# An expert tile's activations transposed between the halves of the next tile's gate and up products

## The chip, the cores and the metric

The kernel runs on one core of a Trainium2 chip. The engines named below are TensorE (PE in the profile, with PEld for its weight loads and PEldq for its sequencer), VectorE (DVE), ScalarE (ACT), GpSimd (POOL) and SyncE (SP). The metric is the device time of one execution in microseconds (us); everything is f32. Before the change three runs took 1644.12, 1644.21 and 1644.91 us, a median of 1644.21 us.

## The reference

The input is one sequence of 2048 tokens of width 512. A Mamba-2 block with a gated MLP is added to the layer-normed input, and then a mixture of experts is added to that. Only the mixture of experts is touched by the change:

```python
x = x + attn_ref(layernorm(x), ...)      # mamba2, then the gated MLP
x = x + ffn_ref(layernorm(x), Wr, Wg, Wu, Wd)
...
probs = softmax(x @ Wr)                  # 8 experts
topk_w, topk_idx = top_k(probs, 2)       # two experts for a token
g = einsum("bsh,ehi->besi", x, Wg)       # h = 512, i = 352
u = einsum("bsh,ehi->besi", x, Wu)
h = silu(g) * u
y = einsum("besi,eih->besh", h, Wd)
out = einsum("bse,besh->bsh", combine, y)
```

The kernel computes only the chosen pairs: 4096 pairs of a token and an expert, sorted by expert and cut into tiles of 128 rows that each belong to one expert. With each expert's last tile padded this makes NS = 39 tiles at most, and the program always runs 39.

## The kernel before

The first 1284 us or so are the Mamba block and the MLP, which the change does not touch. The MLP of the last 512 tokens ends with their routing (`route`, lines 496 to 584: layer norm, router product, the two best experts by VectorE arithmetic, and lists of the pairs). A table of the first eight tiles is made earlier, from the first 1536 tokens; the table of the other 31 (`table`, line 716, called at line 874) needs the end of the routing. Tiles 0 to 6 therefore run beside the routing, and from tile 7 on nothing but tiles is left.

One tile `s` goes through these steps:

- `gather` (line 795): GpSimd issues an indirect DMA that brings 128 token rows into `xg`. `fetch` (line 847) keeps it four tiles ahead.
- `front` (line 803): four transposes of `xg` on TensorE (line 190) into the PSUM tile `pt`, and one ScalarE copy into `xgT` (line 192).
- `hidden` (line 808): the expert's number is loaded into a register of TensorE (line 810), and the gate product `epg` and the up product `epu` are accumulated over four slices `k` of the width, alternating (line 817). Each f32 product of the program appears as two MATMUL records in the trace, so that a tile has 16 of them. ScalarE applies the silu to `epg` (line 819), VectorE multiplies by `epu` (line 820), and the result is `eh`, 128 rows by 352.
- `back` (line 823): three transposes of `eh` on TensorE (line 826, 128, 128 and 96 columns) into the PSUM tile `pht`; VectorE copies two of the three blocks to `ehT` (line 828), ScalarE the third (line 829); three products with the expert's down weights make `epd` (line 832, six MATMUL records); VectorE scales by the pair's weight into `ey` (line 837); GpSimd issues an indirect DMA that adds the rows to `out` (line 838).

`tiles` (line 855) is a generator that writes the steps one tile apart: `hidden(s)` comes before `back(s - 1)`, so that the silu and the multiply of tile `s - 1` lie beside the products of tile `s`:

```python
fetch(s + 1)
...
h = hidden(s, xT.pop(s))
yield
if last and s < NS - 1:
    back(s - 1, *last)
```

The instructions are not issued in exactly this order. A planner puts each engine's instructions in a fixed order when the kernel is built, and it may move work that is ready ahead of work that waits. In the order it made for the steady tiles, TensorE runs, for each `s`: the products of `hidden(s)`, the three transposes of `back(s - 1)`, the four transposes of `front(s + 2)`, and the three products of `back(s - 1)`. At run time each engine goes through its order strictly; an instruction that waits holds up all that follows it on its engine.

Some pools matter. PSUM has two buffers each for `pt` and `pht` (shared), `epg`, `epu` and `epd`. `xgT`, `eh` and `ehT` share one pool of five buffers (`mid`, line 475), from which each tile takes three. `ey` has five buffers, and `xg` five of its own.

Of the kernel before, what the change touches and what calls it, by code (L numbers as in the profile page):

```python
# [36 lines left out]
NS = (2 * T + NE * (P - 1)) // P  # L37
# [11 lines left out]
def mamba_mlp_moe(ctx, tc, x, w_in, w_out, w_gate, w_up, w_down, par, wr, wg, wu, wd, out):  # L49
# [120 lines left out]
    def bank(kind, shape, name):  # L170
        pool, tag = use[kind]
        return pool.tile([P, *shape], F32, name=name, tag=tag)
# [302 lines left out]
    def mid(shape, name):  # L475
        return wk.tile([P, *shape], F32, name=name, tag="mid", bufs=5)
# [158 lines left out]
    def finish(steps):  # L635
        while True:
            try:
                next(steps)
            except StopIteration as end:
                return end.value  # L640
# [75 lines left out]
    def table(n, name, used=None):  # L716


        pn = bank("tr", [NE], f"pn{name}")
        nc.tensor.matmul(pn, ones, before, start=True, stop=True)  # L720
        tiles, upto_e, gt, up8 = small("tiles", NE), small("upto_e", NE), small("gt", NE, NHI), small("up8", NE, NE)
        if used is None:
            nc.vector.tensor_tensor(gt, bc(pn, 2, NHI), bc(count_hi, 1, NE), ALU.is_ge)
            nc.vector.tensor_reduce(tiles, gt, AX.X, ALU.add)
            nc.vector.tensor_scalar_add(tiles, tiles, -1.0)
        else:
            nc.vector.tensor_tensor(gt, bc(pn, 2, NHI), bc(count_hi, 1, NE), ALU.is_gt)
            nc.vector.tensor_reduce(tiles, gt, AX.X, ALU.add)
            nc.vector.tensor_tensor(tiles, tiles, used, ALU.subtract)
# [61 lines left out]
    def of(s):  # L791

        return (s, first, xnd1) if s < NS1 else (s - NS1, rest, xnd)

    def gather(s):
        n, (_, _, idx, _), src = of(s)
        xg = row(f"xg{s}")
        nc.gpsimd.indirect_dma_start(
            out=xg, out_offset=None, in_=src, in_offset=bass.IndirectOffsetOnAxis(ap=idx[:, n : n + 1], axis=0)
        )  # L800
        return xg

    def front(s, xg):
        xT = mid([NK, P], f"xgT{s}")
        transposed(xg, xT)
        return xT

    def hidden(s, xT):
        n, (exp_i, _, _, _), _ = of(s)
        e = nc.tensor.value_load(exp_i[0:1, n : n + 1], min_val=0, max_val=NE - 1)  # L810
        w = ew[:, bass.DynSlice(e, 1), :].rearrange("p a n -> p (a n)")
        pg = bank("g", [EI], f"epg{s}")
        pu = bank("u", [EI], f"epu{s}")
        for k in range(NK):
            for a, ps in enumerate((pg, pu)):
                lo = (2 * k + a) * EI
                nc.tensor.matmul(ps, xT[:, k, :], w[:, lo : lo + EI], start=(k == 0), stop=(k == NK - 1))  # L817
        h = mid([EI], f"eh{s}")
        nc.scalar.activation(h, pg, AF.Silu)  # L819
        nc.vector.tensor_tensor(h, h, pu, ALU.mult)  # L820
        return h, w

    def back(s, h, w):
        pt = bank("tr", [len(ET), P], f"pht{s}")
        for m, (lo, n) in enumerate(ET):
            nc.tensor.transpose(pt[:n, m, :], h[:, lo : lo + n], ident)
        hT = mid([len(ET), P], f"ehT{s}")
        nc.vector.tensor_copy(hT[:, 0:2, :], pt[:, 0:2, :])  # L828
        nc.scalar.copy(hT[: EI - 2 * P, 2, :], pt[: EI - 2 * P, 2, :])
        pd = bank("d", [D], f"epd{s}")  # L830
        for m, (lo, n) in enumerate(ET):
            nc.tensor.matmul(  # L832
                pd, hT[:n, m, :], w[:n, NG + m * D : NG + (m + 1) * D], start=(m == 0), stop=(m == len(ET) - 1)
            )
        y = wk.tile([P, D], F32, name=f"ey{s}", tag="row", bufs=5)
        n, (_, tok_w, idx, _), _ = of(s)
        nc.vector.tensor_scalar_mul(y, pd, tok_w[:, n : n + 1])  # L837
        nc.gpsimd.indirect_dma_start(  # L838
            out=out, out_offset=bass.IndirectOffsetOnAxis(ap=idx[:, n : n + 1], axis=0), in_=y, in_offset=None,
            compute_op=ALU.add,  # L840
        )
# [3 lines left out]
    got, xT = {}, {}  # L845

    def fetch(upto):

        for s in range(min(upto + AHEAD, NS if rest else NS1)):
            if s not in got:  # L850
                got[s] = gather(s)
        if upto in got:
            xT[upto] = front(upto, got[upto])

    def tiles():
        fetch(0)
        last = None
        for s in range(NS):
            fetch(s + 1)
            if last and s == NS - 1:  # L860
                back(s - 1, *last)
            h = hidden(s, xT.pop(s))
            yield
            if last and s < NS - 1:
                back(s - 1, *last)
            last = h
            yield
        back(NS - 1, *last)

    work = tiles()  # L870
    for n, _ in enumerate(feed):
# [70 lines left out]
```

## Time and profile before

One profiled execution took 1643.64 us, with a span of 1641.9 us from its first to its last instruction; 1.74 us lie around the span. The median of the three runs is 0.57 us above the profiled execution.

| What | Value |
|---|---|
| median of the runs | 1644.21 us |
| profiled execution | 1643.64 us |
| its span | 1641.9 us |
| TensorE busy | 1589.6 us, 97% |
| VectorE busy | 706.2 us, 43% |
| ScalarE busy | 597.1 us, 36% |
| GpSimd busy | 299.4 us, 18% |
| mean granted TensorE clock | 0.992 |

The span is read here in four stages, from the timeline. The tiles' first product starts at 1287.43 us. From there to 1353.11 us, where the products of tile 7 start, tiles and routing are mixed. From 1353.11 to 1611.38 us the steady tiles run. From 1611.38 us, where tile 37 starts, the order is that of the end, and the last product of `hidden(38)` is over at 1627.29 us. The rest, 14.6 us, is what follows the last tile's products: silu, multiply, transposes, down products, scaling and the DMA that adds to `out`.

Two habits help in reading it. A MATMUL's duration is not its cost, since the records overlap: a transpose lasts 273 ns, but three of them in a row followed by something else take 0.33 us from start to start. So costs are taken from the starts of neighbouring groups. And a group's idle time is that of its engine just before it, with what ended it.

### The profile page before, as it was taken

What the parts mean: (1) busy time and instruction counts of PE and PEld (TensorE: products, weight loads), DVE (VectorE), ACT (ScalarE), POOL (GpSimd) and SP (SyncE); (2) the same over time, 40 slices, a digit from 0 to 9 for tenths busy, and PEclk for the clock granted to TensorE, in tenths of its full rate; (3) what the DMA queues carried; (4) which work ended last, traced back from release to release, by engine and by line L of the source; (5) the groups of instructions that cost most, each with busy time, mean ns of one, the idle gap of its engine ahead of it and who ended that gap; (6) DMA issues with size and microseconds to landing.
All of it is one profiled execution on the core that took longest, in us unless ns stands there. A gap on an engine that the chain in (4) does not pass through costs nothing.

```text
span 1641.9 us, 16534 instructions
## 1 busy us (share of the span) xinstructions
PE 1589.6 (97%) x5515; PEld 909.0 (55%) x5515; DVE 706.2 (43%) x1835; ACT 597.1 (36%) x1033; POOL 299.4 (18%) x349
## 2 busy tenths in 40 slices
PE   6989899999999999999999999999999999999997
PEld 5656565555556655655565555445444655555553
DVE  6776654534445365535544642323421441111111
ACT  4978774435243533353344334112000211111110
POOL 4332211211021102111201110000010123232221
PEclk9999899999999999999999999999999999999999
DMA  7644333434234533333344321228763234333322
GB/s 250 190 115 130 112 116 113 122 91 122 78 115 129 174 97 90 103 110 109 90 146 150 110 71 58 64 64 265 225 206 116 71 58 73 63 59 63 64 40 32
DMA packets 165203, 182.87 MB, mean 111 GB/s; under 512 B 10432, under 2 KB 125632, under 8 KB 165120
## 3 DMA queue, kind: packets, MB, share of 16 engines
q1 hardware_dynamic: 147456, 145.10, 29.9%
q0 software_dynamic: 8736, 20.45, 7.3%
q10 hardware_dynamic: 8928, 16.26, 2.7%
q8 instruction: 46, 0.75, 0.2%
q14 instruction: 37, 0.30, 0.1%
HBM read 155.04 MB, written 26.74 MB: 111 GB/s over the span
## 4 chain that ended last, share of the span: by engine, by line
PE 85%; DMA 4%; issue 4%; ACT 2%; DVE 2%; POOL 1%; SPq 0%; POOLq 0%; DVEq 0%; ACTq 0%
PE pg L592 13%; PE pd L603 13%; PE pu L592 13%; PE pm L300 9%; PE po L437 6%; PE pz L300 5%; PE epd L832 5%; PE epg L817 4%; PE epu L817 4%; DMA out<-ey,idx 3%; PE py L388 2%; PE psc L361 2%; PE py L382 2%; PE pt L190 2%; PE pls L579 1%
## 5 line engine op out<-in xcount | busy, mean ns | idle before, releaser
L592 PE MATMUL pg<-h2T,mg 128*128 128x512 f32 x512 | 231.8, 593 | 0.0
L592 PE MATMUL pu<-h2T,mu 128*128 128x512 f32 x512 | 230.2, 592 | 0.0
L603 PE MATMUL pd<-md,a 128*128 128x512 f32 x512 | 225.4, 592 | 0.0
L300 PE MATMUL pm<-hT,wi 128*128 128x256 f32 x768 | 183.4, 391 | 0.0
L595 DVE TENSOR_TENSOR a<-a,pu 128x512 f32<-128x512 f32 x64 | 44.0, 688 | 285.3 <-PE pu L592 275.8
L603 PEld LDWEIGHTS pd<-md,a 128*128 128x128 f32 x512 | 97.1, 190 | 122.3 <-issue 120.1
L592 PEld LDWEIGHTS pu<-h2T,mu 128*128 128x128 f32 x512 | 97.2, 190 | 122.0 <-issue 117.9
L300 PEld LDWEIGHTS pm<-hT,wi 128*128 128x128 f32 x768 | 145.8, 195 | 34.0 <-issue 12.6
L592 PEld LDWEIGHTS pg<-h2T,mg 128*128 128x128 f32 x512 | 96.1, 190 | 98.6 <-issue 96.3
L606 DVE TENSOR_TENSOR r<-r,pd 128x512 f32<-128x512 f32 x128 | 87.9, 687 | 116.1 <-PE pd L603 115.2
L319 DVE SCALAR_TENSOR_TENSOR ca<-pre,params,ca 128x256 f32<-128x256 f32 x288 | 129.3, 507 | 0.6
L832 PE MATMUL epd<-ew,ehT 128*128 (+1 forms) x234 | 110.2, 607 | 8.5 <-DVE ehT L828 8.5
L437 PE MATMUL po<-w_o,y 128*128 128x512 f32 x256 | 118.4, 610 | 0.0
L817 PE MATMUL epg<-ew,xgT 128*128 x312 | 118.1, 460 | 0.3 <-ACT xgT L192 0.3
L817 PE MATMUL epu<-ew,xgT 128*128 x312 | 117.7, 459 | 0.0
L300 PE MATMUL pz<-hT,wi 128*128 128x256 f32 x512 | 115.1, 381 | 0.0
L300 PEld LDWEIGHTS pz<-hT,wi 128*128 128x128 f32 x512 | 95.5, 190 | 13.6 <-issue 0.8
L819 ACT ACTIVATE eh<-epg 128x352 f32<-128x352 f32 x39 | 18.1, 465 | 218.7 <-PE epg L817 218.7
L367 ACT ACTIVATE cum<-cum,ncum 128x128 f32<-128x128 f32 x256 | 85.1, 391 | 24.1 <-POOL cum L281 23.5
L594 ACT ACTIVATE a<-pg 128x512 f32<-128x512 f32 x64 | 37.7, 588 | 151.8 <-PE pg L592 134.9
L838 POOL DMA_INDIRECT out<-ey,idx x39 | 61.8, 1584 | 160.3 <-DVE ey L837 146.4
L367 ACT ACT_TABLE_LOAD x65 | 83.4, 1283 | 1.6 <-issue 0.6
(220 smaller groups left out, 1777.1 us busy)
## 6 DMA issues: line engine op xcount, KB each, us to landing
wi<-in_w_in SPq DMA_DIRECT2D x80, 512.0 KB, 3.8
mg<-in_w_gate SPq DMA_DIRECT2D x64, 256.0 KB, 2.9
mu<-in_w_up SPq DMA_DIRECT2D x64, 256.0 KB, 2.9
md<-in_w_down SPq DMA_DIRECT2D x64, 256.0 KB, 2.8
cum<-rowsd SPq DMA_DIRECT2D x32, 512.0 KB, 4.8
ec<-rowsd SPq DMA_DIRECT2D x60, 128.0 KB, 4.1
xnd<-xn ACTq DMA_DIRECT2D x28, 256.0 KB, 3.9
ew<-in_wg SPq DMA_DIRECT2D x8, 704.0 KB, 5.5
```

The source lines that it names most:

```text
L300: nc.tensor.matmul(pm[:, m, :], w[:, k, m * P : (m + 1) * P], hT[:, k, :], start=(k == 0), stop=(k == NK - 1))
L319: nc.vector.scalar_tensor_tensor(ca, pre[:, m, k : k + TB], cw[:, k : k + 1], ca, ALU.mult, ALU.add)
L367: nc.scalar.activation(lt[:, half, i], lt[:, half, i], AF.Exp, bias=ncum[:, j, h : h + 1])
L437: nc.tensor.matmul(po, y[:, m, :], w_o[:, m, :], start=(m == 0), stop=(m == 7))
L592: nc.tensor.matmul(ps, wt[:, k, :], hT[:, k, :], start=(k == 0), stop=(k == NK - 1))
L594: nc.scalar.activation(a, pg, AF.Silu)
L595: nc.vector.tensor_tensor(a, a, pu, ALU.mult)
L603: nc.tensor.matmul(pd, a[:, j * P : (j + 1) * P], d, start=(m == 0), stop=(m == len(held) - 1))
L606: nc.vector.tensor_tensor(rows[j], rows[j], pd, ALU.add)
L817: nc.tensor.matmul(ps, xT[:, k, :], w[:, lo : lo + EI], start=(k == 0), stop=(k == NK - 1))
L832: nc.tensor.matmul(pd, hT[:n, m, :], w[:n, NG + m * D : NG + (m + 1) * D], start=(m == 0), stop=(m == len(ET) - 1))
L838: nc.gpsimd.indirect_dma_start(out=out, out_offset=bass.IndirectOffsetOnAxis(ap=idx[:, n : n + 1], axis=0), in_=y, in_offset=None, compute ...
```

## The change

`hidden` becomes a generator that pauses after the second of its four slices. The transposes and copies of `back` become a function of their own, `turned`, which makes `ehT`; `back` keeps the down products, the scaling and the DMA. `tiles` starts the products of tile `s`, at the pause turns the activations of tile `s - 1`, and then finishes the products (`finish`, line 635, runs a generator to its end and returns its value). For the last tile, `back(s - 1)` is also written at the pause. No arithmetic and no operand changes.

```diff
                 nc.tensor.matmul(ps, xT[:, k, :], w[:, lo : lo + EI], start=(k == 0), stop=(k == NK - 1))
+            if k == 1:
+                yield
         h = mid([EI], f"eh{s}")
         nc.scalar.activation(h, pg, AF.Silu)
         nc.vector.tensor_tensor(h, h, pu, ALU.mult)
         return h, w
 
-    def back(s, h, w):
+    def turned(s, h):
+
         pt = bank("tr", [len(ET), P], f"pht{s}")
         for m, (lo, n) in enumerate(ET):
             nc.tensor.transpose(pt[:n, m, :], h[:, lo : lo + n], ident)
         hT = mid([len(ET), P], f"ehT{s}")
         nc.vector.tensor_copy(hT[:, 0:2, :], pt[:, 0:2, :])
         nc.scalar.copy(hT[: EI - 2 * P, 2, :], pt[: EI - 2 * P, 2, :])
+        return hT
+
+    def back(s, hT, w):
         pd = bank("d", [D], f"epd{s}")
...
             fetch(s + 1)
+            steps = hidden(s, xT.pop(s))
+            next(steps)
+            if last:
+                hT = turned(s - 1, last[0])
             if last and s == NS - 1:
-                back(s - 1, *last)
-            h = hidden(s, xT.pop(s))
+                back(s - 1, hT, last[1])
+            now = finish(steps)
             yield
             if last and s < NS - 1:
-                back(s - 1, *last)
-            last = h
+                back(s - 1, hT, last[1])
+            last = now
             yield
-        back(NS - 1, *last)
+        back(NS - 1, turned(NS - 1, last[0]), last[1])
```

In the order that the planner makes of it, TensorE runs for a steady tile: the first eight MATMUL records of `hidden(s)`, the three transposes of tile `s - 1`, the other eight records, the three down products of tile `s - 1`, and then the four transposes of `front(s + 2)`. For the last two tiles it is: half of `hidden(38)`, the transposes of tile 37, one gate product (two records) of `hidden(38)`, the down products of tile 37, the other six records of `hidden(38)`, and the transposes and down products of tile 38. Up to the transposes of `front(2)`, beside the routing, TensorE's order is unchanged, and so is SP's throughout.

## Prediction

> **What bounds the kernel now.** I read the page's busy shares first, then the waits of the steady tiles, then the timeline of one tile.
>
> ```profile
> PE 1589.6 (97%) x5515; PEld 909.0 (55%) x5515; DVE 706.2 (43%) x1835; ACT 597.1 (36%) x1033; POOL 299.4 (18%) x349
> ```
>
> TensorE sets the time. The page's chain has 3% for the scatter DMA, but that transfer only stands in the chain through inferred releasers: followed closely, its step is VectorE's copy of `ehT`, which had been waiting for other things. So I ask where TensorE stands in the tiles. Of the waits between the down products of 1359.03 and of 1608.70 us (249.67 us), three lines concern TensorE and its weight loads:
>
> ```profile
> PEld epd L832 <- DVE ehT L828: 14.6, 29, 0.8
> PE epd L832 <- DVE ehT L828: 7.7, 29, 0.6
> PEld pht L826 <- issue: 4.5, 29, 0.2
> ```
>
> Every tile's down products wait for the copy of `ehT`; the third line is a load with no waited-for engine, and no other engine makes TensorE wait there. The timeline of one tile shows how much (start, duration, instruction, idle time before):
>
> ```profile
> 1512.33 0.76 PE L817 MATMUL epu<-ew,xgT 128*128 x2
> ...
> 1512.92 0.49 PE L826 MATMUL pht<-ident,eh 128*128 128x128 f32 x3
> ...
> 1513.19 0.52 DVE L820 TENSOR_TENSOR eh<-eh,epu 128x352 f32<-128x352 f32 x1 [4.05 <-PE epu L817]
> 1513.25 0.60 PE L190 MATMUL pt<-ident,xg 128*128 128x128 f32 x4
> 1513.63 0.42 DVE L828 COPY ehT<-pht 128x256 f32<-128x256 f32 x1
> ...
> 1514.10 0.30 PEld L832 LDWEIGHTS epd<-ew,ehT 128*128 128x128 f32 x2 [0.49 <-DVE ehT L828]
> 1514.10 2.85 PE L832 MATMUL epd<-ew,ehT 128*128 x6 [0.25 <-DVE ehT L828]
> ...
> 1516.78 0.76 PE L817 MATMUL epg<-ew,xgT 128*128 x2
> ```
>
> From start to start: the 16 gate and up records from 1508.18 to 1512.92 take 4.74 us; three transposes 0.33; from the four transposes of `front` to the first down product 0.85; the down products 2.68; together 8.60. (30 down groups lie 29 periods apart: 249.67/29 = 8.61.) Where nothing waits, four transposes take 0.43 to 0.44 (fence below), and six down records 2.58 (1312.17 to 1314.75). So a tile loses 0.41 to 0.42 before its down products and 0.10 in them, the latter because the first weight load (it loads `ehT`) cannot run ahead. VectorE is late because it first multiplies the new tile's `eh` (1513.19), then copies.
>
> **The change, part by part.** *The steady tiles.* Removed: the wait. The copy of `ehT` now has the second half of `hidden`, 2.37 us, beside it. It needs, from the first transpose: 0.48 to VectorE's start (1628.14 to 1628.72 in the last tile, where VectorE is free, less the 0.10 of an unprefetched load), 0.42 for it, and 0.04 plus 0.26 on ScalarE for the third block: 1.2 us. If it were uncovered, the old 0.5 would be back. Next in line to be late is the transposes' own operand: `eh` must be done at half of the next `hidden`. Products' end to silu and multiply's end takes about 0.8 (1627.29 to 1628.08), and on TensorE the down products (2.58), four transposes (0.44) and half of `hidden` (2.37) lie between: 5.4 us. What stands behind this moved wait on TensorE is half a `hidden` and the down products, but it has 4.6 us to spare. From the built order the silu now also waits for ScalarE and the multiply for VectorE itself: the five `mid` buffers are taken in another order (`xgT`, `ehT`, `eh`). At worst the buffer is freed by the tile's own last up product, one product pair (0.6 us) later than the silu starts today; the 4.6 us hide it.
>
> Added: no instruction, but new neighbours. `hidden` is entered from transposes twice a tile instead of from down products once. The nearest rows:
>
> ```profile
> 1292.27 0.60 PE L190 MATMUL pt<-ident,xn 128*128 128x128 f32 x4
> 1292.27 0.36 PEld L190 LDWEIGHTS pt<-ident,xn 128*128 128x128 f32 x3 [0.15 <-issue]
> 1292.60 0.30 PEld L817 LDWEIGHTS epg<-ew,xgT 128*128 128x128 f32 x2
> 1292.70 0.76 PE L817 MATMUL epg<-ew,xgT 128*128 x2
> 1293.30 0.76 PE L817 MATMUL epu<-ew,xgT 128*128 x2
> ```
>
> 0.43 us after the transposes' start the gate product starts, and the next product 0.60 after it instead of 0.59: 0.01 lost. The same shows after `pht` (1329.39, 1329.72, 1330.32). I take 0.01 twice. Against it stands a rule of the Trainium skill (TensorE: Matmul & The Clock Gate, Part 3: Packing small matmuls): a weight load overlaps running matmuls only if it aims at another row group. All loads here but the 96-row ones fill every row; by the rule the two new borders, into and out of `pht`, would show their loads, 0.14 and 0.19 us, together 0.33 a tile. By the rows the tile costs 4.74 + 0.33 + 2.58 + 0.44 + 0.02 = 8.11, say 8.10, and saves 0.50; by the rule it saves 0.17. The row decides, since loads of 0.19 already run under products 0.30 apart here; 0.33 is the upper end, and below nothing there is no room, as all else is back to back.
>
> The register load of line 810 moves from behind the down products to behind four transposes. It takes 0.30 + 0.15 + 0.02 = 0.47 us on TensorE's sequencer. In the steady tiles it starts at 1506.1, 2.1 us ahead of its products; at 1298.6 it runs 1.84 ahead of the products of 1300.44 with just such transposes between, and nothing waits. Ahead of it will be 0.44 of transposes and some of the down products; I take nothing, with an upper end in the slow rival.
>
> Of what the moved transposes release, `front`'s copy lands a whole tile before use. GpSimd's gather now becomes ready 0.7 us after the down products' end, just before the scatter does (1.2 after it, 1516.78 to 1518.01): in order, gather (0.98) and then scatter, up to 0.8 us late. The gather is wanted tiles later (it lands in 3.4), and the scatter frees one of five `ey` buffers; two scatters need 5.28 us between them (1621.21 to 1626.49), under 8.1. SP issues nothing here. The savings: 30 tiles (1359.03 to 1608.70) x 0.50 = 15.0 us.
>
> *The end.* From the start of tile 37's products (1611.38) to the end of tile 38's (1627.29) it takes 15.91 now. After: two `hidden` 9.48, two `pht` 0.66, two down groups 5.16, borders 0.02, and the last but one down products, which follow their transposes by only one product pair: 0.33 + 0.59 stand against 0.48 + 0.42 + 0.05, so 0.1 of wait with the unprefetched load. Sum 15.42: 0.5 saved. The 14.6 us behind it stay: after the down products of tile 37 come 1.78 us of products and 5.8 to the last scatter's issue (1627.29 to 1633.11), 7.6 in all, while the scatter before it is issued 1.2 after them and blocks the next one for 5.3, 6.5 in all.
>
> *Beside the routing* (1287.43 to 1353.11, 65.68 us). The same work precedes tile 7's products in both orders. I added up TensorE's costs: 7 `hidden` 33.2, 6 down groups 15.5, 11 groups of four transposes 4.8, 6 `pht` 2.0, routing products 7.9; 63.4. So 2.3 are lost now: two waits for `ehT` about 0.4, for the routing's `v` 0.4, for the second table 0.2, for the first gather of that table 0.8, borders the rest. Walking the new order with these durations, `ehT` and the gather are covered (TensorE has 6.7 us of work between the table's product and that gather's transposes; 5.6 are needed, from 1344.46 to 1350.07). New waits appear where the products between are fewer: about 0.35 at the router product of the last token tile, 0.35 at the second `v`, 0.7 at the table's product, as the scaling of a tile (0.75) is now in VectorE's order before it. A third is open: one `v` waits for TensorE in the built order, 0 to 1.2. I take a saving of 0.5, with ends at -1.0 (a loss) and +1.2.
>
> **Sum.** 15.0 + 0.5 + 0.5 = 16.0: the span goes from 1641.9 to 1625.9, the profiled execution from 1643.64 to 1627.6, and with the 0.57 by which the runs' median lies higher, 1628.2 us.
>
> **The rivals.** *Borders cost more than the row shows.* For: the skill's rule, and a border that no row has in both directions per tile. Against: the rows of 1292 and 1329. At 0.33 a tile 9.9 us are given back: 1638.1.
> *The register load loses its lead, and it gets slower.* Place: the end of each tile's transposes. Price: 0.47 of sequencer and the first pair of loads, 0.30, so 0.77 a tile against 0.50 saved: 31 x 0.27 = 8.4 us over now, less the 1.0 of the other parts: 1651.6. It decides once the sequencer's lead of about 2 us falls under 0.47. For: four transposes last only 0.44. Against: the rows of 1292 and 1300 have exactly this sequence.
> *It does not do what it says.* The planner already moves work; had it moved the transposes back, nothing would change: 1644.2. The built order has them between the halves, so little is left to this; the other way to no change is that the lead is lost in part (0.5 a tile).
>
> **How the numbers follow.** The forecast has 0.85, with its own range of 1626 to 1632: from the routing part (0.7 better to 1.5 worse) and up to 0.08 a tile at the borders. Costly borders 0.08 (1633 to 1640); no change 0.03; slower 0.04. A measurement of this kernel can tell about 0.2%, 3.3 us, from no change. Faster 0.93, same 0.03, slower 0.04. The range goes from 1625.5 to 1633.0, so that costly borders and the rest stay out.
>
> **What would show it.** In the changed profile the steady period should be 8.10 us; the wait of `epd` for `ehT` should be gone but for the end; six down records should take 2.58; `pht` to `epg` should be 0.33; the silu may start 0.6 later after its last gate product; the first product of tile 7 should start near 1352.6. A period of 8.3 or more would point to borders, a gap between `pt` and `epg` to the register load, and a steady period of 8.10 with a late tile 7 to the routing.

## The result, and the profile after

The changed kernel took 1628.03 us (median of five runs, 1627.39 to 1629.27); five runs of the kernel before beside them took 1644.8 us (1644.12 to 1645.2). The ratio is 0.990, with a 95% interval from 0.9887 to 0.9912. The prediction was 1628.2. The two medians lie 16.8 us apart; the spans compared below lie 16.0 apart, which is the saving that was predicted.

The profiled execution is the slowest of the five, with a span of 1627.2 us. The changed kernel was profiled once more later on; that span is 1625.9, the predicted one. From the first page, the busy shares, and the chain by engine:

```profile
PE 1581.5 (97%) x5515; PEld 906.4 (56%) x5515; DVE 706.1 (43%) x1835; ACT 600.2 (37%) x1033; POOL 299.8 (18%) x349
...
PE 90%; ACT 2%; DVE 2%; DMA 2%; issue 2%; POOL 1%; SPq 0%; POOLq 0%; ACTq 0%; DVEq 0%
```

TensorE is busy 97% as before. That share would not have shown the change: the records overlap, so that of the 0.42 lost before the down products of a tile only 0.25 showed as idle time, and the span became shorter with the busy time. The chain does show it, since 90% of it is now TensorE, and 85% was.

The waits of the steady tiles, from 1362 to 1602 us, read engine, line, who ended the wait, then us in total, times and the longest. Two waits of TensorE's weight loads beside one of VectorE:

```profile
DVE ehT L831 <- PE pht L829: 71.5, 30, 2.4
...
PEld epd L838 <- issue: 27.7, 116, 0.2
PEld pt L190 <- issue: 8.6, 30, 0.3
```

No wait of TensorE for `ehT` is left in this stretch. It is VectorE that now waits for the transposes, 2.4 us in each of 30 tiles. The loads' idle stretches of 0.2 are the spacing of products that run back to back. One steady tile of the changed kernel (start, duration, instruction, idle time before):

```profile
1500.06 0.76 PE L817 MATMUL epg<-ew,xgT 128*128 x2
...
1502.43 0.49 PE L829 MATMUL pht<-ident,eh 128*128 128x128 f32 x3
1502.43 0.24 PEld L829 LDWEIGHTS pht<-ident,eh 128*128 128x128 f32 x2 [0.15 <-issue]
1502.65 0.30 PEld L817 LDWEIGHTS epg<-ew,xgT 128*128 128x128 f32 x2
1502.76 0.76 PE L817 MATMUL epg<-ew,xgT 128*128 x2
1502.96 0.42 DVE L831 COPY ehT<-pht 128x256 f32<-128x256 f32 x1 [2.38 <-PE pht L829]
...
1504.80 0.46 ACT L821 ACTIVATE eh<-epg 128x352 f32<-128x352 f32 x1 [1.12 <-PE epg L817]
...
1505.13 2.74 PE L838 MATMUL epd<-ew,ehT 128*128 x6
...
1507.70 0.60 PE L190 MATMUL pt<-ident,xg 128*128 128x128 f32 x4
...
1508.14 0.76 PE L817 MATMUL epg<-ew,xgT 128*128 x2
```

Start to start: half of `hidden` 2.37, transposes 0.33, half of `hidden` 2.37, down products 2.57, `front`'s transposes 0.44, together 8.08. The copy starts 0.53 after the first transpose and is over at 1503.38; the third block is ready 0.3 later, at 1503.68; the down products start at 1505.13. So 1.25 us were needed and 2.70 are there.

Where the 16.0 us between the span of before and that of the second profile lie (both executions have their first tile product at 1287.43 us, and the ends are taken where the next product would start):

| Stage | before | after | saved | predicted |
|---|---|---|---|---|
| first tile product to tile 7's | 65.68 | 65.72 | -0.04 | 0.5 |
| tile 7 to tile 37 | 258.27 | 242.47 | 15.80 | 15.0 |
| tile 37 to the last product of `hidden(38)` | 15.91 | 15.47 | 0.44 | 0.5 |
| what follows | 14.61 | 14.81 | -0.20 | 0 |

The 0.20 at the end belongs to the execution and not to the kernel: in the first profile of the changed kernel what follows took 14.63. In that profile the tiles began 1.02 us later, at 1288.45, behind work that the change does not touch, and tile 6 lost 0.4 once; with the 0.2 less at the end, its span is 1.3 longer.

### The profile page after: what moved, and what is told of

Read it like the earlier page. It is cut to its first block, busy times and chain, and to the rows that moved or that the text cites. A ratio compares the mean times of both kernels' runs of the same rounds, so it can differ in the third digit from the quotient of the medians.

```text
span 1627.2 us, 16530 instructions
## 1 busy us (share of the span) xinstructions
PE 1581.5 (97%) x5515; PEld 906.4 (56%) x5515; DVE 706.1 (43%) x1835; ACT 600.2 (37%) x1033; POOL 299.8 (18%) x349
## 4 chain that ended last, share of the span: by engine, by line
PE 90%; ACT 2%; DVE 2%; DMA 2%; issue 2%; POOL 1%; SPq 0%; POOLq 0%; ACTq 0%; DVEq 0%
PE pg L592 13%; PE pu L592 13%; PE pd L603 13%; PE pm L300 9%; PE po L437 6%; PE epd L838 6%; PE epu L817 6%; PE epg L817 6%; PE pz L300 5%; PE pt L190 2%; PE psc L361 2%; PE py L388 2%; PE py L382 2%; PE pdt L214 1%; PE pl L515 1%
## 5 line engine op out<-in xcount | busy, mean ns | idle before, releaser
L798 POOL DMA_INDIRECT xg<-xnd,idx x39 | 38.3, 981 | 211.7 <-PE pt L190 187.0
```

The lines of the kernel that those rows point to most:

```text
L798: nc.gpsimd.indirect_dma_start(out=xg, out_offset=None, in_=src, in_offset=bass.IndirectOffsetOnAxis(ap=idx[:, n : n + 1], axis=0))
```

## The experiments

In each, the kernel's median stands beside the runs of before from the same chip, and the steady period is the distance from a tile's first product to the next tile's.

**Where the pause stands.** The theory is that the gain is cover: work of TensorE's own that runs while the copies are made. Then any place with more than about 1.2 us from the first transpose to the down products hides them.

```diff
-            if k == 1:
+            if k == 0:      # k0;  k == 2 in k2
```

> The pause comes after the first of the four slices, so that 3.56 us of products lie beside the copy of ehT, and the activations must be ready 1.2 us earlier. Cover theory (the gain is the copy of ehT taken off TensorE's path; any cover over about 1.0 us is as good as another): the steady period stays 8.08 us, the time stays within 1 us of 1628.0 us. Rival (the moved wait for eh takes its place, or the middle is special): a wait before pht appears, the period is over 8.2, the time 1632 us or more.

> The pause comes after the third slice: 1.19 us of products and the 0.33 of the transposes against 1.0 needed from the first transpose to the first down product. Cover theory: period 8.08 us, time within 1 us of 1628.0. Rival (the third block's copy on ScalarE also counts, so that 1.2 to 1.3 us are needed, or the copy suffers beside products): up to 0.1 a tile more, 1631 us.

Pause after the first slice: 1626.92 us (1625.29 to 1627.8), ratio 0.9898 (0.9877 to 0.9919), period 8.082. After the third: 1628.26 us (1627.97 to 1630.19), ratio 0.9906 (0.9886 to 0.9926), period 8.082. Both intervals hold the ratio of the change itself: the middle is no better a place than either of the others.

The limit is found by leaving only one product pair, 0.59 us, behind the transposes:

```diff
-            if k == 1:
-                yield
+                if k == NK - 1 and a == 0:
+                    yield
```

> The pause comes inside the last slice, between its gate and its up product: 0.59 of products and 0.33 of transposes, 0.92 us, against 1.0. Cover theory: about 0.1 of wait and 0.1 of a weight load that cannot run ahead, as at the end of the changed kernel: period 8.28 us, 30 x 0.2 = 6 us more, 1634 us. Rival (the gain comes from leaving the old order, not from the length of cover): 8.08 and 1628.

It took 1634.8 us (1632.69 to 1637.05), ratio 0.9945 (0.9928 to 0.9962), with a period of 8.272. One tile of its timeline:

```profile
1500.39 0.49 PE L829 MATMUL pht<-ident,eh 128*128 128x128 f32 x3
...
1500.72 0.76 PE L817 MATMUL epu<-ew,xgT 128*128 x2
1500.92 0.42 DVE L831 COPY ehT<-pht 128x256 f32<-128x256 f32 x1 [4.16 <-PE pht L829]
...
1501.39 0.30 PEld L838 LDWEIGHTS epd<-ew,ehT 128*128 128x128 f32 x2 [0.48 <-DVE ehT L831]
1501.40 1.55 PE L838 MATMUL epd<-ew,ehT 128*128 x3
```

The wait for `ehT` is back, on the weight load: the down products start 1.01 after the first transpose where the products between end at 0.92, and the first load is not prefetched. That is 0.19 us a tile, as large as the need worked out from durations makes it. The first two blocks decide here, since the third one's product comes later.

**What the borders cost.** Six changes a tile between transposes and products instead of two:

```diff
-            if k == 1:
+            if k < 3:
                 yield
...
             nc.tensor.transpose(pt[:n, m, :], h[:, lo : lo + n], ident)
+            if m < 2:
+                yield
...
```

The lines of `tiles` that call the pieces in turn are left out.

> One of the three transposes after each of the first three slices: three borders between products and transposes in a tile instead of one, and back. The copy still has 1.19 us of products and 0.11 of a transpose beside it. Row theory (a border costs about 0.01 us): period 8.08 to 8.12, time 1628 to 1629.5. Rule of the skill (the weight loads into and out of a border show, 0.14 and 0.19): 0.66 more a tile, 8.74 and 1648 us.

It took 1627.99 us (1627.43 to 1629.4), ratio 0.9904 (0.9883 to 0.9924), period 8.087. Four more borders cost 0.005 us together. The timeline shows why:

```profile
1500.81 0.14 PEld L829 LDWEIGHTS pht<-ident,eh 128*128 128x128 f32 x1
1501.10 0.27 PE L829 MATMUL pht<-ident,eh 128*128 128x128 f32 x1
1501.10 0.30 PEld L817 LDWEIGHTS epg<-ew,xgT 128*128 128x128 f32 x2 [0.15 <-issue]
1501.21 0.76 PE L817 MATMUL epg<-ew,xgT 128*128 x2
```

The transpose's load is over 0.15 before the transpose starts, under the product that still runs, and the next product's loads begin with the transpose. All these operands fill 128 rows. The rule weighed in the prediction, that a load overlaps only products in other row groups, would have given 8.74.

**What the copy costs, and what the old wait was made of.** VectorE copies its two blocks twice, once in the changed kernel and once in the old one; then ScalarE takes the two blocks and VectorE the third in the old kernel.

```diff
         nc.vector.tensor_copy(hT[:, 0:2, :], pt[:, 0:2, :])
+        nc.vector.tensor_copy(hT[:, 0:2, :], pt[:, 0:2, :])   # copy2_after, copy2_before
```

```diff
-        nc.vector.tensor_copy(hT[:, 0:2, :], pt[:, 0:2, :])   # swap_before
-        nc.scalar.copy(hT[: EI - 2 * P, 2, :], pt[: EI - 2 * P, 2, :])
+        nc.scalar.copy(hT[:, 0:2, :], pt[:, 0:2, :])
+        nc.vector.tensor_copy(hT[: EI - 2 * P, 2, :], pt[: EI - 2 * P, 2, :])
```

> The changed kernel with VectorE's copy into ehT done twice, 0.42 us more. Cover theory: 1.45 us are needed and 2.7 are there (2.37 of products, 0.33 of transposes), so the period stays 8.08 us and the time within 1.5 us of 1628.0. Rival (the copy is still on the path): 0.42 a tile, 13 us, 1641.

> The kernel before with VectorE's copy into ehT done twice. The planner, which counts a longer wait here, puts the next tile's first gate product (0.60 us) between the transposes and the down products. Cover theory: from the first transpose 0.71 + 0.42 + 0.42 + 0.05 = 1.6 us are needed, 0.33 + 0.44 + 0.60 = 1.37 are there: 0.23 of wait and 0.1 of a load, 0.33 instead of 0.52 a tile, so more copying makes it FASTER, by about 6 us: 1639 us, period 8.41. Rival (VectorE's and ScalarE's work itself is what costs): 0.42 a tile more, 1657 us.

> The kernel before, with ScalarE copying the two blocks and VectorE the third, so that the first copy does not queue behind VectorE's multiply of the next eh. If the queue on VectorE is part of the old wait (0.18 of the 0.52 a tile: 0.71 against 0.53 from the first transpose to the copy's start), the period falls from 8.60 to between 8.35 and 8.42 and the time to 1637 to 1640 us. If the multiply has no part in it: 8.60 and 1644.8.

In the changed kernel it took 1628.45 us (1627.2 to 1629.75), ratio 0.9906 (0.9889 to 0.9922), with a period of 8.082: in the steady tiles the second copy costs nothing. At the end, where nothing covers it, it does. The last tile's down products in the changed kernel (second profile), then with the second copy, and what two stretches around the latter show (after the busy times of the engines, the third number from the end is the granted clock):

```profile
1613.01 2.85 PE L838 MATMUL epd<-ew,ehT 128*128 x6 [0.52 <-DVE ehT L831]
...
1613.47 4.54 PE L839 MATMUL epd<-ew,ehT 128*128 x6 [0.97 <-DVE ehT L832]
...
1611.00:1614.00 3.00, 1.34 (x5) 0.59 (x5) 1.37 (x3) 0.44 (x2) 1.55 (x1) 0.97 0.30 11
1614.00:1616.00 2.00, 2.00 (x4) 0.78 (x3) 0.00 (x0) 0.00 (x0) 0.00 (x0) 0.50 0.64 115
```

The copy itself costs 0.45 there. Behind that longer wait the granted clock fell to 0.50, and the six records took 1.7 us longer. The same happened in the other kernel with two copies (4.54 us again), and in none of the twelve other profiles (2.84 to 2.85). So an uncovered copy can cost more than its own length.

In the old kernel the second copy makes the kernel no slower: 1642.28 us (1640.35 to 1644.19), ratio 0.999 (0.9981 to 0.9999), period 8.464 against 8.60. The direction was as expected, the size was not (8.41 and 1639): 0.29 of wait is left in a tile instead of 0.23, and the 2.1 us at the end, which the expectation did not have, take back half of what the steady tiles gain. The added copy led the planner to another order:

```profile
1502.44 0.52 DVE L820 TENSOR_TENSOR eh<-eh,epu 128x352 f32<-128x352 f32 x1 [3.46 <-PE epu L817]
1502.49 0.60 PE L190 MATMUL pt<-ident,xg 128*128 128x128 f32 x4
...
1502.88 0.42 DVE L828 COPY ehT<-pht 128x256 f32<-128x256 f32 x1
1502.93 0.76 PE L817 MATMUL epg<-ew,xgT 128*128 x2
...
1503.33 0.42 DVE L829 COPY ehT<-pht 128x256 f32<-128x256 f32 x1
...
1503.81 0.70 PE L833 MATMUL epd<-ew,ehT 128*128 x1
```

The next tile's first gate product now stands between the transposes and the down products. The down products start 0.88 after that product, where 0.59 is the spacing without a wait. One product pair, 0.59 us of cover, is worth more in a steady tile than a whole copy costs.

With the copies exchanged it took 1637.82 us (1636.71 to 1639.79), ratio 0.9968 (0.9955 to 0.998), period 8.369 in the order of the old kernel:

```profile
1501.31 0.49 PE L826 MATMUL pht<-ident,eh 128*128 128x128 f32 x3
...
1501.58 0.52 DVE L820 TENSOR_TENSOR eh<-eh,epu 128x352 f32<-128x352 f32 x1 [4.05 <-PE epu L817]
1501.63 0.60 PE L190 MATMUL pt<-ident,xg 128*128 128x128 f32 x4
1501.83 0.37 ACT L828 COPY ehT<-pht 128x256 f32<-128x256 f32 x1 [0.46 <-PE pht L826]
...
1502.26 0.30 PEld L832 LDWEIGHTS epd<-ew,ehT 128*128 128x128 f32 x2 [0.26 <-ACT ehT L828]
```

The copy no longer stands behind the multiply of 1501.58, and 0.23 of the old loss of 0.52 are gone: most of it because the copy starts 0.52 after the first transpose instead of 0.71, and the rest because ScalarE's copy takes 0.37 where VectorE's takes 0.42. The other 0.29 remain: 0.44 us of transposes is too little cover for this copy too.

**Whether the register load matters.** The slower rival said that the expert's number, loaded on TensorE's sequencer, loses its lead. First it is loaded three times (two of the values are not used), then at the pause of the tile before:

```diff
+        for _ in range(2):                                     # load3, in hidden
+            nc.tensor.value_load(exp_i[0:1, n : n + 1], min_val=0, max_val=NE - 1)
...
```

```diff
             next(steps)
+            load_number(s + 1)                                 # hoist, in tiles
...
```

The function `load_number`, left out here, holds the load of `hidden` and keeps its result; `hidden` loads only what has not been loaded yet.

> The changed kernel with the expert's number loaded three times for a tile; two of the loads are not used. That is about 1 to 1.4 us more of TensorE's sequencer. If the sequencer's lead of 4.2 us in the steady tiles is real cover, the steady period stays 8.08; beside the routing, where one load had a lead of only 0.8 us and the product behind it came 0.43 late, that gap grows by about 1 us or more: 1629 to 1630.5. Rival (the load is on the path in the steady tiles): 0.5 to 1 a tile, 1643 to 1660 us.

> The changed kernel with the expert's number of tile s + 1 loaded at the pause of tile s. Beside the routing the first gate product of tile 2 came 0.43 us late behind its register load. If the load's lost lead is the cause, that gap closes, the stretch from the first product to tile 9's first product goes from 81.9 to about 81.5 us, and the steady period stays 8.08: 1627.6 us. If not, 81.9 and 1628.0.

Three loads: 1633.84 us (1631.42 to 1634.05), ratio 0.9937 (0.992 to 0.9953). The steady period stays 8.082, as expected: from tile 8 on even three loads are hidden. The stretch beside the routing became 5.3 us longer where about 1 was expected. Part of it is the gap in front of a gate product, 0.36 us in each of two rows like the second here, and part are longer waits for VectorE like the first. About 1.7 us are neither: behind a wait of 0.67 for `xT` the granted clock fell to 0.50 (third row, again the third number from the end), and four groups of products and transposes from 1306.29 on took 4.23 us instead of 2.46. No other profile has such a stretch beside the routing, and whether the added loads caused it is not shown. How the rest divides was not separated.

```profile
1327.72 1.13 PE L579 MATMUL pls<-v,ohl 128*128 128x256 f32 x4 [0.80 <-DVE v L577]
1329.21 0.85 PE L819 MATMUL epg<-ew,xgT 128*128 x2 [0.36 <-issue]
...
1308.00:1310.00 2.00, 2.00 (x6) 1.41 (x5) 1.73 (x11) 1.29 (x2) 0.00 (x0) 0.50 0.85 88
```

The early load: 1625.92 us (1624.81 to 1626.81), ratio 0.9896 (0.9879 to 0.9912), period 8.082. It is the lowest median of all kernels here, but these runs do not tell it from the changed kernel. The profile does: the routing stretch is 64.65 us, against 65.7 in both profiles of the changed kernel and in that of k0. That is 1.05 saved, more than the 0.4 expected, which had counted one gap only. So the gap was closed alone, by loading early for tile 2 only, and the changed kernel was profiled again:

```diff
             next(steps)
+            if s == 1:                                         # hoist_one
+                load_number(2)
...
```

> The changed kernel itself, profiled a second time. The first profile lost 0.38 us at the down products of tile 6 (1359.54 us), where VectorE's copy came late; five variants with the same order there did not show it. If it is a chance of that one execution: the stretch from the tiles' first product to tile 9's first product is 81.9 us (first profile 82.3), and no wait shows near 1359. If it belongs to this kernel: 82.3 again. Both: steady period 8.08, the gap of 0.86 us between the transposes of xn near 1305.4 and tile 2's first product is there again, time 1627 to 1629 us.

> As the version that loads every tile's expert number at the pause of the tile before, but for tile 2 alone. That version gained 1.05 us beside the routing, of which the one measured gap, at tile 2, is only 0.43. If that gap is the cause and moves all that follows it: a stretch from the first product to tile 9's first product of 80.8 us, as there, with the waits for xT (0.7) and sel (0.5) gone too. If the rest came from the other tiles' loads: 81.4 to 81.5 with those waits still there. Steady period 8.08; time 1626 to 1628 us.

The changed kernel took 1628.02 us, one run. The late copy of tile 6 did not come again: the stretch to tile 9's first product is 81.88, so the 0.4 of the first profile belonged to that execution. The gap did come again, here in the changed kernel:

```profile
1304.30 0.42 PEld L190 LDWEIGHTS pt<-ident,xn 128*128 128x128 f32 x4 [0.65 <-issue]
1304.33 0.63 PE L190 MATMUL pt<-ident,xn 128*128 128x128 f32 x4
...
1305.15 0.30 PEld L817 LDWEIGHTS epg<-ew,xgT 128*128 128x128 f32 x2 [0.43 <-issue]
1305.16 0.85 PE L817 MATMUL epg<-ew,xgT 128*128 x2 [0.20 <-issue]
```

and here closed, with the load for tile 2 alone made early:

```profile
1303.94 0.63 PE L190 MATMUL pt<-ident,xn 128*128 128x128 f32 x4
...
1304.30 0.30 PEld L824 LDWEIGHTS epg<-ew,xgT 128*128 128x128 f32 x2
1304.41 0.76 PE L824 MATMUL epg<-ew,xgT 128*128 x2
```

From transposes to product it is 0.83 us with the gap and 0.47 without. With it the product pair also takes 0.69 to the next group instead of 0.60. Still the routing stretch is 65.66, no shorter (1626.95 us, one run), and the expectation was missed both ways. The planner had put another router product one product pair earlier, and it waited there for ScalarE's copy:

```profile
1294.97 0.76 PE L824 MATMUL epu<-ew,xgT 128*128 x2
1295.23 0.59 ACT L192 COPY xT<-pt 128x512 f32<-128x512 f32 x1 [2.53 <-DMA xnd<-xn]
1295.86 0.97 PEld L515 LDWEIGHTS pl<-wr_sb,xT 128*128 128x128 f32 x8 [0.70 <-ACT xT L192]
```

The router product starts 0.89 after the product ahead of it instead of 0.59, and its own loads come late: 0.4 lost for 0.4 gained, against the second profile of the changed kernel, which reaches the transposes in front of tile 2 16.90 us after the first tile product where this one needs 17.30. The kernel with all loads early has the same 0.4 loss, and gets its 1.05 later on, where TensorE no longer waits for `sel` (0.49) and `v` (0.21). Whether those two go because of the loads or of the order that came with them stays open.

**The end.** The early place for the down products of tile 37 is taken away:

```diff
-            if last and s == NS - 1:
-                back(s - 1, hT, last[1])
...
-            if last and s < NS - 1:
+            if last:
                 back(s - 1, hT, last[1])
```

> The changed kernel without the special place of the last but one tile's down products: they follow the last tile's products, as in every other tile. They then cover the last silu and multiply, for which TensorE stands 0.85 us in the changed kernel. If the scatter chain decides the end (two scatters at least 5.3 us apart), the last scatter is issued 6.5 us after these down products, 0.5 us later than now: from tile 38's first product to the last scatter's issue 14.2 us instead of 13.7, time 1628.5. If the chain of products and copies decides it: 12.6 us, time 1627.

It took 1627.78 us (1627.09 to 1628.73), ratio 0.9909 (0.9893 to 0.9926). The last two scatters on GpSimd:

```profile
1611.51 1.55 POOL L844 DMA_INDIRECT out<-ey,idx  x1 [6.09 <-DVE ey L843]
1617.02 1.55 POOL L844 DMA_INDIRECT out<-ey,idx  x1 [3.96 <-DMA out<-ey,idx]
```

The last one waits for the transfer of the one before, 5.51 us from issue to issue. From tile 38's first product (1602.63) to that issue it takes 14.39 us, and 13.66 in the changed kernel, whose last scatter waits for `ey` and not for the other scatter. So the spacing of scatters does decide once the down products of tile 37 are late, and the early place is worth 0.7 us, too little for the medians to show.

## Why the prediction was right, by its steps

**The steady wait.** Right in place and size. A period of 8.10 was predicted and 8.082 measured, so 0.51 go instead of 0.50. Thirty tiles gave 15.80 rather than 15.0. About half of the difference is that 0.51; the other half is that the profiled execution of before also held one tile of 8.95 us (`ehT` late by a further 0.35 near 1419.5), which the sum had not counted. That cover is the cause is shown from four sides: the position does not matter (k0, k2), too little cover brings back the predicted remainder (k3half), a doubled copy is free when covered (copy2_after), and one product pair of cover shortens the steady tile of the old kernel in spite of a second copy (copy2_before). That TensorE keeps its order shows in the kernel before: the gate products of 1516.78 had their `xgT` from 1505.88 on, and still stood behind the wait that ended at 1514.10.

**The borders.** The row was right, and even its 0.01 was too much: 0.005 for four more. The other end, 0.33 a tile from the Trainium skill (TensorE: Matmul & The Clock Gate, Part 3: Packing small matmuls), does not hold for these loads.

**Next in line.** `eh` was in time, with the 4.6 us of room that were worked out (1505.90 for 1510.51). The silu was feared 0.6 late because of the changed order of buffers; it came 0.07 later after its gate product than before, so that worst case did not occur. The gather is ready first and is issued at 1500.50, and the scatter follows it 0.3 after the gather's end, at 1501.79: in the order predicted, and free.

**The register load.** In the steady tiles nothing was lost, as taken. It starts 4.3 us ahead (1503.87 for 1508.14), earlier than the working had it, and lasts 0.63 to 0.74 us in three neighbouring tiles instead of 0.30. The slower rival's mechanism is real, but only at one place of the changed kernel: at tile 2 the load stands behind transposes that wait for `xn`. It starts at 1304.35 with them, and its product starts 0.81 later. That 0.8 is what the way from a load's start to its product takes at least: it is 0.79 in both rows with a gap in the kernel with three loads, and 0.81 at tile 7 in the first profile, where the load starts 0.37 ahead of the transposes and leaves no gap. The rival's price of 0.77 (0.47 of sequencer, 0.30 of weight loads) was close. At tile 2, with only 0.44 of transposes beside it, it leaves the gap of 0.37. The prediction had applied its safe row (1.84 us of lead) to every tile, and had not asked where the transposes ahead of a load would wait themselves.

**Beside the routing.** This is the term that failed: 0.5 predicted, none measured (-0.04, inside its ends of -1.0 and +1.2). The gather's wait (0.62) went as predicted. Of the three new waits, that at the table's product is there with 0.49 of idle time (0.7 predicted), and one for `v` with 0.21 and its late loads (0.35 predicted); the first, at the router product of the last token tile, came to 0.1 at most (0.35 predicted). The gap at tile 2, which was in no step, is about as large as what is missing. It is not shown to be the cause: closing it alone gained nothing, since the planner spent the gain elsewhere.

**The end.** 0.44 against 0.5: the wait for `ehT` and the late weight load come to 0.19 where 0.1 was counted. The scatters do not collide, as worked out. Without the early down products they would, by 0.7. The 5.28 us that two scatters were said to need is not a fixed need: k0 has two 5.14 apart.

The sum hit this closely because errors of opposite sign cancelled: 0.8 more in the steady tiles, against 0.5 less beside the routing and 0.2 less behind the last products, and part of the 0.8 and all of the 0.2 belong to single executions. So the agreement to 0.2 us is luck; what was right is the steady wait, with nearly all of the saving. The spread of five runs alone is 1.9 us.

## What to carry to other kernels

When an in-order engine waits in every round for a copy of its own result, measure what the copy needs from the first instruction that feeds it, and put that much independent work of the same engine between; more was worth nothing here, and where it stood was free. A border between two kinds of work can be priced by a row in which it already occurs. A register load inherits every wait ahead of it in its queue: ask for each place, not for the steady one alone, and read the whole built order, because a planner may give back elsewhere what one edit gains.

## What the runs showed that was not expected

The register load lasts 0.30 us in the steady tiles of the kernel before, and up to 0.93 in those of the changed kernel, without a loss. How busy TensorE is does not explain it: the loads for tiles 9 to 33 take 0.61 to 0.93 us, and those for tiles 34 to 37, amid the same products, 0.30. The long ones start 3.4 us after a gather is issued; the last gather is issued at 1557.07, and the first short load follows at 1568.52. With the pause after the first slice (k0) the load starts 2.3 us after the gather and takes 0.30 at the same tiles, but 0.38 to 0.41 at tiles 34 to 37. That the gather lengthens it fits most of these times, and no run tests it.

Two scatters that add to the same tensor were never issued closer than 5.14 us here. Where a scatter was held up by the one before, it was issued 5.44 to 5.81 us after it.

And an execution can lose some tenths at one place only: the copy of `ehT` came late once in the first profile of the changed kernel (tile 6) and once in that of before (there behind a multiply that was itself late), and not in the second profile of the changed kernel. What held it up stays open.
